# Four banks of depthwise results put into rows by two engines: which engine takes which bank, and in which order

## The chip, the cores and the metric

The kernel runs on one core of one Trainium2 chip. The core has five engines that run side by side and wait for each other through semaphores: TensorE (PE in the profile; its weight loads are PEld), VectorE (DVE), ScalarE (ACT), GpSimd (POOL) and SyncE (SP, which starts transfers). TensorE writes its results into PSUM, 8 banks of 512 float32 values in each of 128 partitions; ScalarE and VectorE read them from there. SBUF is the memory for everything else on the chip. The metric is the device time of the whole program in microseconds, from one launch.

## What is computed

Four layers follow each other, each added to its input: `x = x + layer(group_norm(x))`, with x of shape 2 x 128 x 64 x 64 (two images, 128 channels). Only layer 0 is touched. Its heart, cut from the reference:

```python
xn = biasfree_ln(x, ln1_w)
qkv = conv1x1(xn, w_qkv)                        # 128 -> 640 channels, "pointwise"
qkv = conv_general_dilated(qkv, w_dw, ...,      # 3 x 3, each channel by itself, "depthwise"
                           padding='SAME', feature_group_count=5 * c)
q1, k1, v, q2, k2 = split(qkv, 5, axis=1)       # 128 channels each
q1, q2, k1, k2 = map(l2norm_tokens, (q1, q2, k1, k2))
attn1 = softmax(q1 k1^T * temperature)          # over the 4096 pixels, 4 heads of 32 channels
out1 = attn1 v
...                                             # channel attention with q2, k2
out = conv1x1(out1 + out2, w_po) ; layer norm ; conv1x1 with w_proj
```

The change concerns how the depthwise results of k1 and q1 get from PSUM into their places in SBUF. No number that is computed changes.

## The kernel before

In layer 0 each group of 128 channels is convolved in two halves of 32 image rows. The pointwise product goes through PSUM into a padded frame in SBUF; the depthwise product works on that frame with 32 x 32 pieces of TensorE: channels `32 r .. 32 r + 31` are multiplied by a diagonal matrix for each of 9 taps, and the result for chunk c (8 image rows, 512 pixels) of channel block r lands in partitions `32 c .. 32 c + 31` of bank r. So the results of four chunks lie in the four quarters of the partitions and have to be put back into rows: that is `in_place`.

```python
def sp():                                # 3 buffers of two PSUM banks each
    return spp.tile([128, 2, CH], F32, tag="sp", name="ps_sp")      # CH = 512
...
def pointwise(pad, grp, half):           # a generator: one yield for each block
    ...                                  # memsets of the frame's edges on GpSimd
    for r0 in range(0, H // 2 + 1, 2 * ROWS):          # 16 rows, 16 rows, 1 row
        n = min(2 * ROWS, H // 2 + 1 - r0)
        ps = sp() if n > 1 else acc(0).rearrange("p (o c) -> p o c", o=1)
        for i in range(0, n, ROWS):
            ...
            nc.tensor.matmul(ps[:, i // ROWS, : rows * W], w_qkv[...], xn[...], start=True, stop=True)   # L1524
        nc.scalar.copy(pad[:, to + r0 : to + r0 + n, 1 : W + 1], ...)                                    # L1531
        yield

def depthwise(grp, pad):
    ps = [sp() for _ in range(2)]
    for t in range(9):
        for c in range(4):
            for r in range(4):
                rows, to = slice(32 * r, 32 * r + 32), slice(32 * c, 32 * c + 32)
                y0 = c * ROWS + t // 3
                nc.tensor.matmul(                                                                        # L1546
                    ps[r // 2][to, r % 2, :].rearrange("p (h w) -> p h w", w=W),
                    diag[rows, grp, t, :],
                    pad[rows, y0 : y0 + ROWS, t % 3 : t % 3 + W],
                    start=(t == 0), stop=(t == 8),
                )
    return ps
...
def in_place(ps, half, out, p):
    for c in range(4):
        for r in range(2 * p, 2 * p + 2):
            cols = slice((4 * half + c) * CH, (4 * half + c + 1) * CH)
            (nc.vector.tensor_copy if r % 2 else nc.scalar.copy)(                                        # L1564
                out[32 * r : 32 * r + 32, cols], ps[p][32 * c : 32 * c + 32, r % 2, :]
            )
```

`convolutions` runs eight steps per image, in the order k1, k1, q1, q1, then q2 and k2 by halves. Each step's program order is the order on every engine (`_in_order`):

```python
order = [(1, 0), (1, 1), (0, 0), (0, 1), (3, 0), (4, 0), (3, 1), (4, 1)]
...
for n, (grp, half) in enumerate(order):
    ps = depthwise(grp, frames.pop(0))
    ...
        following = pointwise(frames[-1], *order[n + 2])     # the frame for the step after next
    if grp >= 3:                                             # q2, k2: whole tiles, rows not undone
        for p in range(2):
            copy(qk[:, grp - 3, 2 * p : 2 * p + 2, :], ps[p])                                            # L1557
        run(following)
        ...
    else:                                                    # k1, q1
        in_place(ps, half, out, 0)
        next(following, None)                                # first pointwise block
        in_place(ps, half, out, 1)
        run(following)                                       # second block, and the single row
        for i in range(2):
            squares(...)                                     # ScalarE, sums of squares                    L1571
    if n == 0:
        for half in range(2):
            run(pointwise(pads[half], 2, half))              # the frames of v
        for _ in range(6):
            next(before, None)                               # finish() of the image before
    elif n == 1:
        run(before)
    ...
    if n == 3: ...                                           # norms of q1 and k1
    for _ in range((0, 0, 3, 3, 4, 4, 4, 0)[n]):
        next(taps, None)                                     # VectorE: depthwise taps of v
```

`finish` of the first image (output projections, transposes, layer norm) is woven into the first two steps of the second image.

Of the kernel before, what the change touches and what calls it, by code (L numbers as in the profile page):

```python
# [1406 lines left out]
def _layer0(ctx, tc, X, a, cst, worst, there, dram):  # L1407
    nc = tc.nc
# [149 lines left out]

    def in_place(ps, half, out, p):

        for c in range(4):
            for r in range(2 * p, 2 * p + 2):
                cols = slice((4 * half + c) * CH, (4 * half + c + 1) * CH)
                (nc.vector.tensor_copy if r % 2 else nc.scalar.copy)(  # L1564
                    out[32 * r : 32 * r + 32, cols], ps[p][32 * c : 32 * c + 32, r % 2, :]
                )

    def squares(pool, t, at):
        junk = pool.tile([128, 2 * CH], F32, tag="junk", name="junk", bufs=1)
# [57 lines left out]
    def convolutions(pool, b, before):  # L1627
# [12 lines left out]
        for n, (grp, half) in enumerate(order):  # L1640
# [5 lines left out]
            if grp >= 3:  # L1646
                if grp == 3:
                    qk = pool.tile([128, 2, 4, CH], F32, tag="qk2", name="qk2", bufs=1)
# [4 lines that stand above are left out]
                    squares(pool, qk[:, grp - 3, r, :], ss2[:, grp - 3, r, half : half + 1])  # L1653
            else:
                out = (q1, k1)[grp]
                in_place(ps, half, out, 0)
                next(following, None)
# [3 lines that stand above are left out]
                    at = 2 * half + i  # L1661
                    squares(
                        pool, out[:, at * 2 * CH : (at + 1) * 2 * CH], ss[:, grp, at : at + 1]
                    )
# [677 lines left out]
```

## Time and profile before

| | |
|---|---|
| median of three runs | 4260.06 us (4249.1 to 4260.55) |
| span of the profiled run | 4250.7 us |
| TensorE busy | 4058.6 us, 95% of the span |
| ScalarE busy | 3342.0 us, 79% |
| VectorE busy | 2187.2 us, 51% |
| copies of line 1564 on ScalarE | 64, median 577 ns, 37.0 us in all |
| copies of line 1564 on VectorE | 64, 687 to 688 ns on average, 44.0 us in all |
| mean granted TensorE clock | 0.978 of full speed |

Layer 0's convolutions stand near 40 to 210 us (first image) and 827 to 1045 us (second image); between and after them lies attention, in which TensorE and ScalarE are both nearly always busy. A group of the profile names the line, the engine, the operation, the tile written and the tile read, the shape and how often. "Idle before, releaser" is the time for which an engine stood still just before an instruction, and the instruction that ended that. Idle time matters only on an engine that sets the end.

### The profile page before, as it was taken

The page shows a single profiled execution, that of the slowest core. Times are in us where ns is not written, and L with a number is a line of the kernel's source. Part 1 is how long each engine was busy: PE and PEld are TensorE (multiplying, and loading weights), DVE is VectorE, ACT ScalarE, POOL GpSimd, SP SyncE. Part 2 cuts the span into 40 slices and gives each one's busy share as a digit, 9 for nine tenths or more (in the row PEclk, how much of TensorE's full clock was granted, in tenths as well). Part 3 has the DMA queues.
Part 4 walks back from the last instruction along what each step waited for, and adds up shares of the span by engine and source line. Part 5 has one row for each costly group of instructions (what it writes and reads, how often), then busy time and mean ns, then how long its engine had stood idle before and what let it go on. Part 6 is the DMA issues. An engine that isn't in the chain of part 4 may idle for free. (4 is left out here: it accounts for less than half of the span.)

```text
span 4250.7 us, 82260 instructions
## 1 busy us (share of the span) xinstructions
PE 4058.6 (95%) x35790; PEld 1552.1 (37%) x35790; DVE 2187.2 (51%) x2358; ACT 3342.0 (79%) x4051; POOL 70.4 (2%) x145
## 2 busy tenths in 40 slices
PE   7899999978999998997998999999999999999998
PEld 4523222245222223445665333333333333333332
DVE  3679999746999998986765211321032012211111
ACT  4478888734888884335655999999999999999998
POOL 1001000000000001000000000000000000000000
PEclk9999999999999999998999999999999999999999
DMA  1099970000000000003660000000000000000000
GB/s 48 2 194 191 182 89 1 1 1 2 1 1 1 1 1 12 1 1 128 270 263 4 6 6 4 6 6 4 6 6 6 4 6 6 6 4 6 6 6 4
DMA packets 158822, 158.86 MB, mean 37 GB/s; under 512 B 24809, under 2 KB 148713, under 8 KB 154354
## 3 DMA queue, kind: packets, MB, share of 16 engines
q1 hardware_dynamic: 158450, 153.50, 15.5%
q8 instruction: 282, 4.62, 0.4%
q14 instruction: 90, 0.74, 0.1%
HBM read 145.09 MB, written 73.40 MB: 51 GB/s over the span
## 5 line engine op out<-in xcount | busy, mean ns | idle before, releaser
L2104 ACT ACTIVATE weights<-ps_s 128x1024 f32<-128x1024 f32 x2048 | 1885.2, 1103 | 65.9 <-PE ps_s L2094 65.4
L1350 ACT ACTIVATE weights<-ps_s 128x1024 f32<-128x1024 f32 x1024 | 992.6, 1022 | 175.5 <-PE ps_s L1341 150.6
L2113 PE MATMUL ps_acc<-weights,vt 128*32 128x512 f32 x8192 | 1095.6, 607 | 0.0
L2094 PE MATMUL ps_s<-q,k 32*128 32x512 f32 x8192 | 925.9, 445 | 5.3 <-ACT weights L2104 5.3
L1792 DVE TENSOR_TENSOR sums<-sums,weights 128x2048 f32<-128x2048 f32 x384 | 879.1, 2289 | 42.2 <-ACT weights L1350 6.6
L2094 PEld LDWEIGHTS ps_s<-q,k 32*128 32x128 f32 x8192 | 472.6, 183 | 841.9 <-ACT weights L2104 775.2
L1341 PE MATMUL ps_s<-q,k 32*128 32x512 f32 x4096 | 647.4, 642 | 3.7 <-ACT weights L1350 1.3
L2135 DVE COPY u<-ps_acc 128x512 f32<-128x512 f32 x32 | 22.1, 692 | 1041.5 <-PE ps_acc L2113 1041.5
L1757 PE MATMUL ps_acc<-weights,vt 128*32 128x512 f32 x4096 | 548.8, 605 | 3.4 <-ACT used L1782 3.2
L1341 PEld LDWEIGHTS ps_s<-q,k 32*128 32x128 f32 x4096 | 210.4, 183 | 429.7 <-issue 209.9
L2113 PEld LDWEIGHTS ps_acc<-weights,vt 128*32 128x32 f32 x8192 | 163.2, 108 | 378.8 <-issue 366.8
L1757 PEld LDWEIGHTS ps_acc<-weights,vt 128*32 128x32 f32 x4096 | 81.0, 108 | 395.1 <-issue 377.0
L662 DVE SCALAR_TENSOR_TENSOR X<-g,w,X 128x2048 f32<-128x2048 f32 x84 | 197.4, 2351 | 2.6
L1792 DVE TENSOR_TENSOR sums<-weights 128x2048 f32<-128x2048 f32 x64 | 146.6, 2290 | 63.1 <-ACT weights L1350 63.1
L1546 PE MATMUL ps_sp<-pad,diag 32*32 32x512 f32 x4608 | 165.3, 600 | 4.6 <-DVE q L1564 3.1
L1008 PE MATMUL ps_z<-w_ri,e 128*32 128x128 f32 x2048 | 137.5, 409 | 14.4 <-DVE e L950 12.2
L2055 DVE TENSOR_TENSOR vt<-ps_acc,bv 128x384 f32<-128x384 f32 x32 | 17.8, 557 | 247.1 <-PE ps_acc L2048 247.1
L1524 PE MATMUL ps_sp<-xn,w_qkv 128*128 128x512 f32 x160 | 91.3, 709 | 33.5 <-DVE k L1564 16.0
L1546 PEld LDWEIGHTS ps_sp<-pad,diag 32*32 32x32 f32 x4608 | 95.1, 103 | 62.6 <-issue 15.4
L2025 DVE LOAD_MASK_SELECT qq<-ps_acc x32 | 0.4, 14 | 222.2 <-PE ps_acc L2022 222.2
L2138 DVE RECIPROCAL r<-r 128x512 f32<-128x512 f32 x32 | 107.3, 3353 | 1.1
L950 DVE TENSOR_SCALAR e<-ps_pe 32x136 f32<-32x136 f32 (+1 forms) x352 | 104.4, 297 | 5.0
(288 smaller groups left out, 2602.6 us busy)
## 6 DMA issues: line engine op xcount, KB each, us to landing
w_ri<-w_r SPq DMA_DIRECT2D x16, 2112.0 KB, 8.2
w_ri<-w_i SPq DMA_DIRECT2D x16, 2112.0 KB, 13.5
w_r<-in_L_conv_kr_w SPq DMA_DIRECT2D x15, 528.0 KB, 12.5
w_r<-in_L_conv_kr_x SPq DMA_DIRECT2D x15, 528.0 KB, 12.2
w_r<-in_L_conv_kr_y SPq DMA_DIRECT2D x15, 528.0 KB, 12.1
w_r<-in_L_conv_kr_z SPq DMA_DIRECT2D x15, 528.0 KB, 12.4
w_i<-in_L_conv_ki_w SPq DMA_DIRECT2D x15, 528.0 KB, 12.7
w_i<-in_L_conv_ki_x SPq DMA_DIRECT2D x15, 528.0 KB, 12.2
```

The costliest lines, as they stand in the source:

```text
L662: nc.vector.scalar_tensor_tensor(xi, g[:, i : i + H // 2, j : j + W], w8[:, s : s + 1], xi, ALU.mult, ALU.add)
L950: nc.vector.tensor_scalar_mul(out, got[of, :, s], sign)
L1008: nc.tensor.matmul(out.rearrange("p (n f o) -> p n f o", n=2, f=2), e[:, s, 2 * j : 2 * j + 2, :].rearrange("p f x -> p (f x)"), w.rearran ...
L1341: nc.tensor.matmul(ps[j // 2][:, j % 2, :], k[rows, kt * 128 : (kt + 1) * 128], q[rows, qb * CH : (qb + 1) * CH], start=True, stop=True,)
L1350: nc.scalar.activation(w[:, 2 * p : 2 * p + 2, :], ps[p], AF.Exp)
L1546: nc.tensor.matmul(ps[r // 2][to, r % 2, :].rearrange("p (h w) -> p h w", w=W), diag[rows, grp, t, :], pad[rows, y0 : y0 + ROWS, t % 3 : t ...
L1757: nc.tensor.matmul(ac[n][rows, :], lhs(rows), w[:, j, :], start=first, stop=last)
L1792: nc.vector.tensor_add(parts[0].rearrange("p j c -> p (j c)"), t.rearrange("p j c -> p (j c)"), w.rearrange("p j c -> p (j c)"),)
L2094: nc.tensor.matmul(ps[j // 2][:, j % 2, :], k[rows, kt * 128 : (kt + 1) * 128], q[n][rows, qb * CH : (qb + 1) * CH], start=(n == 0), stop= ...
L2104: nc.scalar.activation(w[p], ps[p], AF.Exp)
L2113: nc.tensor.matmul(ac[0][32 * j : 32 * j + 32, :], vt[:, kt, j // 2, i : i + 2, :].rearrange("p a d -> p (a d)"), w[j // 2][:, i, :], star ...
L2138: nc.vector.reciprocal(r, r)
```

## The change

Before, `in_place(…, p)` handles tile p: its bank 0 goes to ScalarE, its bank 1 to VectorE, chunk by chunk, the same chunk of columns on both. After, ScalarE takes both banks of the first tile and VectorE both banks of the second: call p moves bank p of each tile. VectorE begins two chunks ahead, so the two engines never write the same columns at the same time. The aim is that each engine works through a tile of its own.

```diff
     def in_place(ps, half, out, p):
 
-        for c in range(4):
-            for r in range(2 * p, 2 * p + 2):
+
+        for i in range(4):
+            for n, engine in enumerate((nc.scalar.copy, nc.vector.tensor_copy)):
+                r, c = 2 * n + p, (i + 2 * n) % 4
                 cols = slice((4 * half + c) * CH, (4 * half + c + 1) * CH)
-                (nc.vector.tensor_copy if r % 2 else nc.scalar.copy)(
-                    out[32 * r : 32 * r + 32, cols], ps[p][32 * c : 32 * c + 32, r % 2, :]
-                )
+                engine(out[32 * r : 32 * r + 32, cols], ps[n][32 * c : 32 * c + 32, p, :])
```

The copies are as many as before and of the same shape, eight on each engine in each of the four steps of an image.

## The prediction, made before the changed kernel was run

> **What bounds the kernel now.** I read the page first. TensorE is busy 95% of the span, and in the slices that hold layer 0's convolutions (slice 0 and slices 8 to 9) it is as busy as elsewhere, so any gain has to come out of TensorE's waits there. The group list of line 1564, the line that changes, shows who waits for it:
>
> ```profile
> L1564 ACT COPY k<-ps_sp x32: 573/577/580, 58.1 to 911.1; 32x512 f32<-32x512 f32 x32
> L1564 DVE COPY k<-ps_sp x32: 680/686/698, 58.7 to 911.8; 32x512 f32<-32x512 f32 x32
> ...
> who waited for it (us, times):
>   DVE k L1564: 82.8, 32
>   DVE q L1564: 46.6, 32
>   PE ps_sp L1524: 30.0, 8
> ...
>   PEld ps_sp L1546: 8.8, 5
>   PE ps_sp L1546: 3.9, 5
> ```
>
> Columns of the first lines are shortest/median/longest ns. The two engines wait for each other at every copy, and TensorE's lines 1524 (pointwise) and 1546 (depthwise) wait for the copies. The eight waits of line 1524 are one for each of the eight calls of the depthwise step that end in `in_place`: four per image. The timeline of the second of them, from the end of its depthwise matmuls at 84.53, shows the whole pattern (start us, duration us, engine, line, operation; in brackets idle before it and what ended that idle):
>
> ```profile
> 84.53 1.98 PE L1524 MATMUL ps_sp<-xn,w_qkv 128*128 128x512 f32 x4
> 84.60 0.57 ACT L1564 COPY k<-ps_sp 32x512 f32<-32x512 f32 x1 [8.69 <-PE ps_sp L1546]
> 85.21 0.68 DVE L1564 COPY k<-ps_sp 32x512 f32<-32x512 f32 x1 [16.16 <-ACT k L1564]
> 85.93 0.58 ACT L1564 COPY k<-ps_sp 32x512 f32<-32x512 f32 x1 [0.75 <-DVE k L1564]
> ...
> 89.19 1.01 ACT L1531 COPY pad<-ps_sp 128x1024 f32<-128x1024 f32 x1
> 89.20 0.69 DVE L1564 COPY k<-ps_sp 32x512 f32<-32x512 f32 x1 [0.65 <-ACT k L1564]
> ...
> 90.04 3.13 PE L1524 MATMUL ps_sp<-xn,w_qkv 128*128 128x512 f32 x4 [3.52 <-DVE k L1564]
> ...
> 94.83 0.70 DVE L1564 COPY k<-ps_sp 32x512 f32<-32x512 f32 x1 [0.65 <-ACT k L1564]
> ...
> 95.58 9.72 PE L1546 MATMUL ps_sp<-pad,diag 32*32 32x512 f32 x284 [0.80 <-DVE k L1564]
> ```
>
> ScalarE and VectorE never overlap on these copies: one pair costs 1.33 us (84.60 to 85.93). Four pairs must end before TensorE may start the second pointwise block (90.04), four more before the next depthwise block runs (95.58). Depthwise end to depthwise start is 95.58 - 84.53 = 11.05 us. A step without `in_place` shows what the same TensorE work takes when nothing holds it:
>
> ```profile
> 146.62 3.70 PE L1524 MATMUL ps_sp<-xn,w_qkv 128*128 128x512 f32 x8
> 150.16 0.33 PE L1524 MATMUL ps_acc<-xn,w_qkv 128*128 128x64 f32 x2
> 150.42 1.14 PE L1546 MATMUL ps_sp<-pad,diag 32*32 32x512 f32 x32
> ```
>
> There the gap is 150.42 - 146.62 = 3.80 us. So 7.25 us of such a gap is waiting, or slow matmuls after waiting.
>
> **What the Trainium skill says.** "PSUM — Partial Sum Buffer", section on PSUM bank collisions: ScalarE and VectorE must be kept apart where they touch one bank in the same 32 partitions; different banks are free. The old pair already read two different banks, so the alternation is not needed by the banks; it comes from both engines reading one and the same two-bank tile (at the first copy after the tile changes, ScalarE waits for nobody). The order of instructions with their waits, of both kernels, confirms it: in the changed kernel no copy waits for the other engine any more. Same page, Specifications: both engines read PSUM at full bandwidth together when they don't collide. The trace agrees: whole-tile copies of line 1557 take 1.01 us on ScalarE and 1.22 on VectorE when they run together (186.41 and 186.54), as long as when alone. "TensorE: Matmul & The Clock Gate", What's actually happening: about 3.4 us of idleness drops TensorE to half clock. The trace agrees: after 3.52 us idle the four matmuls at 90.04 took 3.13 us, after 1.16 us (907.19) 1.98 us; after 2.14 us (836.81), partly slow, 2.45.
>
> **The change part by part.** Instruction counts, shapes and TensorE's order stay the same; eight copies per engine and step remain.
>
> Removed: the cross waits. ScalarE's own rate is read from line 691, the same 32x512 copy sixteen times in a row: 9.45 us / 16 = 0.591 each. VectorE's is its 0.687 plus the same 0.014, 0.70.
>
> Moved: the release of buffers. Before, the first tile was free after half the copies; now both are free only at the end. But the order of releases becomes: the buffer of the first pointwise block (free when its copy to the pad is done), then ScalarE's tile, then VectorE's. I take it that buffers are handed out in order of release, as the waits of both kernels fit. So the second pointwise block no longer waits for depthwise copies at all, only for ScalarE's pad copy, which stands after ScalarE's first four copies.
>
> One step, counted from the depthwise end:
> - ScalarE: starts at 0.08, four copies to 0.08 + 4 x 0.591 = 2.45, pad copy 1.02 to 3.47, four more to 5.85.
> - TensorE: first pointwise 0 to 1.98, waits for the pad copy to 3.53 (1.55 idle instead of 3.52, so I expect full speed), second pointwise 1.85, small one 0.26 (both from the free step: 150.16 - 146.62 is 3.54 for two, and 150.42 - 150.16), ends at 5.64.
> - VectorE: starts near 0.2, eight copies of 0.70, ends at 5.8.
> - Next depthwise block: first tile is ScalarE's (5.85), second VectorE's (5.8), with about 0.1 for the handover: 5.95.
>
> So 11.05 becomes 5.95: 5.1 us less. Such gaps are the second, third and fourth step of the first image and the third and fourth of the second: 5 x 5.1 = 25.5 us.
>
> First step of each image (a value pad follows): depthwise ends at 58.06, the next starts at 74.85, 16.79 us. ScalarE is the last there: its squares began at 69.36, after alternating to 68.33, and the value-pad copies follow the squares. ScalarE now finishes copies at 5.85, pad copy 2 at 6.97, squares near 7.1 instead of 11.30. Everything behind them moves by 4.2 us. Twice: 8.4, of which I count 8 since the second image has the latency chain of `finish` behind it, which moves along but may not move whole.
>
> Second step of the second image: a tile of `finish` holds the third buffer, so the first pointwise block waits even now (5.43 us idle, until 902.28). It will then wait for VectorE's eight copies, 5.8: no gain. But the second block need not wait for the pad copy and the transposes that started at 912.51, 15.7 us after the depthwise end, come after 5.8 + 3.75 (slow) + 1.98 + 0.33 = 11.9, or when ScalarE's tile is free: pad copy 9.6 to 10.6, four copies to 13.0. Gain 2.6 to 3.8, I take 3.
>
> Added: in step four the squares end later relative to the next depthwise block, and with them VectorE's norm and its three taps, so the copy of line 1557 (already 1.8 us late at 148.44) comes about 0.9 later; some 0.3 us each, -0.6.
>
> Sum: 25.5 + 8 + 3 - 0.6 = 36 us, out of layer 0 only; attention and the later layers keep their durations and start earlier. Against the median of 4260.06 this gives 4224; against the lowest run, 4249.1, it gives 4213. I say 4221.
>
> **The rivals.** (a) *The later release takes the gain back.* If the second pointwise block gets ScalarE's tile instead of the pad's buffer, it waits until 5.9, longer than the 5.5 of before, TensorE goes slow (3.4 us), and the next depthwise block starts near 9.7. Gain 1.4 x 5 + 8 + 1 = 16 us, 4243. For it: the waits listed name only the engine (ScalarE), which fits both. Against it: in the kernel before, the third step's first tile waits for ScalarE and starts early (93.42), which only a hand-out in order of release explains. (b) *Copies slow each other.* If both engines at once take 20% longer, each step loses about 1.1 us: 5 x 1.1 + 2 x 1 = 8 us of the gain, 4230. Line 1557 speaks against it. (c) *The end is elsewhere.* If the second image's `finish` chain or a weight load set the pace, the gain there vanishes: about 11 us less, 4232. The waits of line 1524 stand on the chain of TensorE, 95% busy, so I give this little. (d) *More gain:* VectorE's successive copies overlap by 0.08 (as line 1833 starts 0.61 after line 1470's 0.69), or `finish` gains more: up to 42 us, 4216.
>
> **Range and chances.** (a) at its worst, with the spread of 11 us of the runs before, gives about 4245; the full gain from the lowest run with some more gives 4205. Low 4204, high 4240. 2% would be 85 us; all waits for line 1564 on TensorE together are 43 us with slow matmuls on top, so 2% can't be reached: faster 0.02, same 0.97, slower 0.01.
>
> **What would show it.** Right: no waits between ScalarE and VectorE on the copies; eight VectorE copies in a row in about 5.6 us; the wait of line 1524 near 1.5 us and its four matmuls 1.98; depthwise gaps of 6 us, 12.5 in the first step. Rival (a): line 1524 idles about 4 us and takes over 3. Rival (b): copies longer than 0.577 and 0.687. Wrong altogether: if depthwise gaps shrink as said but the span does not.

## The result, and the profile after

The changed kernel takes 4225.19 us (median of 4 runs, 4223.08 to 4228.96), the kernel before 4255.27 us (median of 4 runs beside it): a ratio of 0.9928 with a 95% interval of 0.9913 to 0.9943. That is 30 us less, where the prediction said 36 and a time of 4221, range 4204 to 4240. In the profiled runs the span went from 4250.7 to 4221.3 us, at a mean granted TensorE clock of 0.978 and 0.980.

The group list of the line that changed (now line 1566) answers to the one shown of before. Durations are shortest/median/longest ns, then first and last start.

```profile
L1566 ACT COPY k<-ps_sp x32: 575/578/581, 59.2 to 888.4; 32x512 f32<-32x512 f32 x32
L1566 DVE COPY k<-ps_sp x32: 681/688/698, 59.3 to 880.9; 32x512 f32<-32x512 f32 x32
...
its engine sat idle before it (us, times) until:
  PE ps_sp L1546: 156.6, 16
who waited for it (us, times):
  PE ps_sp L1524: 6.3, 3
  PE ps_sp L1546: 1.6, 5
  PEld ps_sp L1524: 0.7, 2
```

The copies last what they lasted before, and no copy waits for the other engine: all 16 waits ahead of copies are for TensorE's depthwise matmuls. TensorE's line 1524 waited for these copies 8 times and 30.0 us; now it is 3 times and 6.3 us, nearly all of it one wait of 5.80 us in the second image. The other seven waits became waits of 1.51 to 1.53 us for the copy to the pad, which this list does not hold.

The timeline of the second depthwise step, from the end of its matmuls at 82.19 (start us, duration us, engine, line, operation; in brackets the idle time before it and what ended it):

```profile
82.19 1.98 PE L1524 MATMUL ps_sp<-xn,w_qkv 128*128 128x512 f32 x4
82.27 2.35 ACT L1566 COPY k<-ps_sp 32x512 f32<-32x512 f32 x4 [8.69 <-PE ps_sp L1546]
82.33 5.61 DVE L1566 COPY k<-ps_sp 32x512 f32<-32x512 f32 x8 [17.43 <-PE ps_sp L1546]
...
84.64 1.01 ACT L1531 COPY pad<-ps_sp 128x1024 f32<-128x1024 f32 x1
85.67 2.36 ACT L1566 COPY k<-ps_sp 32x512 f32<-32x512 f32 x4
...
85.70 1.98 PE L1524 MATMUL ps_sp<-xn,w_qkv 128*128 128x512 f32 x4 [1.52 <-ACT pad L1531]
...
87.52 0.33 PE L1524 MATMUL ps_acc<-xn,w_qkv 128*128 128x64 f32 x2
...
88.18 1.16 PE L1546 MATMUL ps_sp<-pad,diag 32*32 32x512 f32 x32 [0.32 <-ACT k L1566]
```

Both engines start together and each runs through its own tile. The second pointwise block waits 1.52 us for the copy to the pad, not 3.52 us for VectorE, and its four matmuls take 1.98 us, not 3.13. The next depthwise block starts 88.18 - 82.19 = 5.99 us after the last one's end, not 11.05.

The windows over the first image's convolutions tell how much of the gain is waiting and how much is clock (columns: window, its length, busy us of PE, PEld, DVE, ACT and POOL with instruction counts, then TensorE's granted clock, share of the DMA engines, GB/s). First before, then after:

```profile
40.00:211.00 171.00, 148.84 (x2558) 86.09 (x2556) 77.48 (x70) 69.51 (x121) 4.26 (x26) 0.94 0.01 2
```

```profile
40.00:191.00 151.00, 138.01 (x2557) 82.54 (x2556) 77.01 (x70) 70.23 (x121) 4.75 (x26) 1.00 0.01 2
```

TensorE's idle time fell from 22.2 to 13.0 us, 9.2 less. The same matmuls keep it busy for 10.8 us less, and not all of that is clock, though the clock rose from 0.94 to 1.00. Line 1524 is busy for 5.0 us less (46.33 to 41.33) and lines 1608 and 1618 for 1.9 us less (17.63 to 15.76); before, these ran slow after waits. Line 1546 is busy for 3.5 us less (82.54 to 79.09), and most of that is waiting under another name: before, three depthwise blocks began with four matmuls alone, 1.36, 1.15 and 1.05 us long, while the other 284 waited for VectorE. The last 0.5 us is where the windows are cut. So of 20 us gained here about a third is clock. The part of lines 1608 and 1618 need not come from the change: the wait ahead of them is 3.08 us in both kernels, and in the second image they ran slow in both.

### The profile page after: what moved, and what is told of

The parts are those of the page before. It is cut to its first block, busy times and chain, and to the rows that moved or that the text cites. A ratio compares the mean times of both kernels' runs of the same rounds, so it can differ in the third digit from the quotient of the medians.

```text
span 4221.3 us, 82246 instructions
## 1 busy us (share of the span) xinstructions
PE 4050.3 (96%) x35790; PEld 1548.6 (37%) x35790; DVE 2186.7 (52%) x2358; ACT 3342.7 (79%) x4051; POOL 71.6 (2%) x145
## 5 line engine op out<-in xcount | busy, mean ns | idle before, releaser
L948 ACT ACTIVATE e<-ps_pe 32x136 f32<-32x136 f32 (+1 forms) x352 | 99.4, 282 | 4.1
## 6 DMA issues: line engine op xcount, KB each, us to landing
w_r<-in_L_conv_kr_y SPq DMA_DIRECT2D x15, 528.0 KB, 12.3
```

## The experiments

Ten runs, each with the change or the kernel before as its base. "Step" is one depthwise block with what follows it; "gap" is the time from the end of a depthwise block to the start of the next.

**Without the distance of two chunks.** Base: after.

```diff
-                r, c = 2 * n + p, (i + 2 * n) % 4
+                r, c = 2 * n + p, i
```

> The changed kernel without the two chunks' distance: both engines write the same columns (other rows) at the same time. Theory (a tile of its own for each engine ends the waiting; the distance does nothing): no waits between the copies, 0.578 and 0.688 us each, gap from depthwise end to depthwise start 5.97 us as in the changed kernel, ratio to before 0.993. Rival (the distance is needed, because equal columns hold one engine up): copies longer than 0.6 and 0.7 us or waits back, gap above 6.5 us, ratio 0.995 to 1.000.

Measured: 4224.1 us, ratio to before 0.9924 (0.9908 to 0.9941), the same as the change. The second step's gap is 5.99 us (81.15 to 87.14), the copies take 578 and 688 ns. What follows: the distance does nothing that shows, and the gain comes with the tile that each engine has for itself.

**The distance without the own tile.** Base: before. Both engines still read one tile, VectorE two chunks ahead.

```diff
-        for c in range(4):
+        for i in range(4):
             for r in range(2 * p, 2 * p + 2):
+                c = (i + 2 * (r % 2)) % 4
```

> The kernel before with the two chunks' distance alone: VectorE's bank two chunks ahead, both engines still on one tile. Theory (the shared tile makes them alternate): all waits stay, pair 1.33 us, gap 11.05 us, ratio 1.000. Rival (equal columns make them alternate): waits gone, gap near 6 us, ratio 0.993.

Measured: 4257.19 us, ratio 1.0003 (0.9994 to 1.0012). The timeline of its second step shows the wait of before:

```profile
90.19 3.75 PE L1524 MATMUL ps_sp<-xn,w_qkv 128*128 128x512 f32 x4 [3.52 <-DVE k L1565]
```

VectorE's copies into k again wait 82.8 us for ScalarE in 32 waits, to the tenth what they waited before (those into q 48.2 us, where it was 46.6). Together the two runs settle what made the engines alternate: they read one tile. The columns they write play no part.

**All copies before the first pointwise block.** Base: after. Here ScalarE's tile and VectorE's are both ahead of the pad copy in the order of release, which makes a case like the one that rival (a) described.

```diff
                 in_place(ps, half, out, 0)
-                next(following, None)
                 in_place(ps, half, out, 1)
+                next(following, None)
                 run(following)
```

> The changed kernel with all copies ahead of the first pointwise block in program order, so that ScalarE's tile is released before the pad's buffer and its pad copy comes last. Theory (the order in which buffers come free is a part of the gain): the second pointwise block waits for ScalarE's eighth copy, starts at 4.9 us instead of 3.5 after the depthwise end, idle 2.9 us before it, gap 7.0 us at full TensorE clock and up to 8.5 when the clock drops; 6 to 12 us of the 30 are lost, 4231 to 4237 us. Rival (only the parallel copies count): gap 6.0 us, as the changed kernel.

Measured: 4233.65 us, ratio 0.9945 (0.9928 to 0.9961): some 9 us slower than the changed kernel (4225.19, and 4224.1 without the distance). TensorE's timeline of the second and the fourth step:

```profile
83.88 1.98 PE L1524 MATMUL ps_sp<-xn,w_qkv 128*128 128x512 f32 x4
88.70 1.98 PE L1524 MATMUL ps_sp<-xn,w_qkv 128*128 128x512 f32 x4 [2.84 <-ACT k L1566]
90.53 0.33 PE L1524 MATMUL ps_acc<-xn,w_qkv 128*128 128x64 f32 x2
90.78 9.77 PE L1546 MATMUL ps_sp<-pad,diag 32*32 32x512 f32 x288
...
117.09 1.98 PE L1524 MATMUL ps_sp<-xn,w_qkv 128*128 128x512 f32 x4
121.93 3.47 PE L1524 MATMUL ps_sp<-xn,w_qkv 128*128 128x512 f32 x4 [2.86 <-ACT q L1566]
...
125.50 9.76 PE L1546 MATMUL ps_sp<-pad,diag 32*32 32x512 f32 x288
```

Now the second pointwise block waits for a tile of depthwise results, 2.84 to 2.86 us, and in these two steps its matmuls once stayed fast and once ran slow: gaps of 6.90 and 8.41 us. So the second block takes the buffer that was released first, as the prediction supposed; in the change that is the pad's, and this order is worth some 9 of the 30 us. The traces agree: from the end of the first depthwise block to the start of the attention, the two images take 7.0 and 3.1 us more than in the change.

**The squares later.** Base: after. In the first step ScalarE's sums of squares stand behind the pointwise blocks of the value pads, not ahead of them.

```diff
                 in_place(ps, half, out, 1)
                 run(following)
+            if n == 0:
+                for h in range(2):
+                    run(pointwise(pads[h], 2, h))
+            if grp < 3:
                 for i in range(2):
                     squares(...)
             if n == 0:
-                for half in range(2):
-                    run(pointwise(pads[half], 2, half))
                 for _ in range(6):
```

> The changed kernel with ScalarE's sums of squares behind the value-pad copies in the first step of each image. Theory after the trace (TensorE's own pointwise matmuls set that step, 7.46 us without a wait after the copies): first gap 13.35 us as before this edit. Theory of the prediction (ScalarE sets it): squares moved out of the way, gap 11 us.

Measured in a single run: 4207.31 us. But the first gap, which this edit is about, is the same as in the change to the hundredth: 13.35 us.

```profile
57.64 1.99 PE L1524 MATMUL ps_sp<-xn,w_qkv 128*128 128x512 f32 x4
...
70.99 1.47 PE L1546 MATMUL ps_sp<-pad,diag 32*32 32x512 f32 x33
```

So ScalarE does not set the end of the first step after the change, and the 18 us of the whole must come from elsewhere. In the trace, 8.4 us of them lie behind the second image's convolutions (3200.2 us to the end of the span, in the change 3208.6) and 3.6 us in the first image's attention (617.2 against 620.8), which the edit does not touch. The kernel was run again; the 14 us that the expectation names fit this run's time set against the changed kernel's span of 4221.3 us:

> The same edit as in the one look before, timed, because that look ended 14 us below the changed kernel although the gap that the edit aims at was the same 13.35 us. Theory (the 14 us came from stretches in which TensorE happened to be granted a higher clock, 0.984 against 0.980 over the whole run, and are no effect of the edit on layer 0): layer 0's gaps as in the changed kernel; the time between 4215 and 4228, ratio 0.991 to 0.993. Rival (the edit itself brings it): 4205 to 4210, ratio 0.989.

Measured: 4216.93 us, with runs from 4208.07 to 4221.98, ratio 0.9908 (0.9886 to 0.993), whose interval overlaps the change's. Its profiled run has the same gap, 13.34, and a span of 4220.2 us at a clock of 0.979, where the single run had 4205.5 at 0.984. One kernel, 15 us apart: a single whole time says nothing about an edit of a few microseconds here. If a small gain hides in the 4217, this doesn't tell.

**Finish runs nine steps in the first, not six.** Base: after. `finish` of the first image then holds no two-bank buffer while it pauses for the second step's depthwise block; with six steps it holds one of the three.

```diff
-                for _ in range(6):
+                for _ in range(9):
                     next(before, None)
```

> The changed kernel with nine instead of six steps of finish in the first step of the second image, so that no tile of finish holds the third buffer in the second step. Theory (that buffer costs the second step 5.8 us of waiting and slow matmuls after it): from the first depthwise end to the third depthwise start of the second image 73.65 us become 66 to 68, the first pointwise block of the second step starts at once, the time falls to 4217 to 4220, ratio 0.991 to 0.992. Rival (finish's own chain of latencies sets that stretch, and the moved steps cost the same elsewhere): 73 us stay, ratio 0.993.

Measured: 4212.16 us (4212.03 to 4214.46), ratio 0.9897 (0.988 to 0.9913), 13 us faster than the change: this version beats both kernels. From the end of the first depthwise block of the second image to the start of the third it takes 896.61 - 832.18 = 64.43 us; in the change it is 906.26 - 832.61 = 73.65. First the change, then this kernel, both from TensorE's timeline:

```profile
865.44 10.48 PE L1546 MATMUL ps_sp<-pad,diag 32*32 32x512 f32 x288
881.72 6.46 PE L1524 MATMUL ps_sp<-xn,w_qkv 128*128 128x512 f32 x8 [5.80 <-DVE k L1566]
...
888.18 0.60 PE L1816 MATMUL ps_sp<-consts,y 128*128 128x128 f32 x4
890.17 1.12 PE L1821 MATMUL ps_acc<-yn,w_pr 128*128 128x512 f32 x2 [1.38 <-ACT pad L1531]
...
904.29 2.04 PE L1821 MATMUL ps_acc<-yn,w_pr 128*128 128x512 f32 x2 [0.94 <-DVE X L1833]
906.26 10.51 PE L1546 MATMUL ps_sp<-pad,diag 32*32 32x512 f32 x288
```

```profile
876.00 9.77 PE L1546 MATMUL ps_sp<-pad,diag 32*32 32x512 f32 x288
885.70 1.98 PE L1524 MATMUL ps_sp<-xn,w_qkv 128*128 128x512 f32 x4
889.21 1.98 PE L1524 MATMUL ps_sp<-xn,w_qkv 128*128 128x512 f32 x4 [1.53 <-ACT pad L1531]
...
895.55 1.13 PE L1821 MATMUL ps_acc<-yn,w_pr 128*128 128x512 f32 x2 [1.68 <-ACT yn L1818]
896.61 9.76 PE L1546 MATMUL ps_sp<-pad,diag 32*32 32x512 f32 x288
```

In the change the held buffer costs an idle of 5.80 us and then eight matmuls at 6.46 us; without it both blocks run at full speed and the tail of `finish` as well. The first step grows by 11 us for it, the second shrinks by 20. That is 9.2 of the 13 us; about 4 lie outside this stretch and are not explained.

**The same nine steps with the old copies.** Base: before.

> The kernel before with nine instead of six steps of finish in the first step of the second image. Theory (the held buffer is a cost of its own, and part of it hides behind alternating copies): from the first depthwise end to the third depthwise start of the second image 78.63 us become about 73, the gaps stay 11.05, the time falls by 5 to 6 us, ratio 0.9987. Rival (the whole 9.2 us that the nine steps brought on the changed kernel come back): 69.4 us, ratio 0.9978. Rival (the nine steps help only the changed kernel): 78.6 us, ratio 1.000.

Measured: 4254.03 us against 4250.65 of before, ratio 1.0009 (1.0 to 1.0018). In the profile the stretch shrinks from 78.63 to 73.19 us, as expected, and the next attention starts at 1039.34, not 1043.36; but the time doesn't show it. Right behind the stretch 1.7 us are given back, since the third depthwise block takes 11.46 us, not 9.76. The runs spread over 17 us (4242.31 to 4259.39), and where the rest of the 5 us went stays open.

**Eleven steps.** Base: after, `range(11)`: all of `finish` in the first step.

> The changed kernel with all eleven steps of finish in the first step of the second image. Theory (with nine, the last two steps cost 5 us in the second step, with waits for ScalarE's squares; in the first step they cost their own latencies of some 4 us): the second step's gap becomes 6 us, the stretch of 64.43 us becomes 63 to 64.5, the time equals that of nine steps, 4211 to 4213, ratio 0.989 to 0.990. Rival (latencies of the last steps are fully exposed in the first step): 68 us, 4216.

Measured: 4220.64 us, ratio 0.993 (0.9913 to 0.9947), above both expectations; the stretch is 66.78 us, between the two. So the stretch explains 2.4 of the 8.5 us by which this kernel is slower than the one with nine steps; in the two profiles 6.3 us lie behind the second image's convolutions, which the edit does not touch. The last steps of `finish` are a chain from engine to engine with no second chunk beside it, as the idle before its last transposes shows:

```profile
875.93 1.11 PE L1816 MATMUL ps_sp<-consts,y 128*128 128x128 f32 x4 [2.47 <-DVE y L1470]
880.72 9.76 PE L1546 MATMUL ps_sp<-pad,diag 32*32 32x512 f32 x288
```

With nine steps this tail lies beside the second step's copies. So more is not always better: of the three counts run, nine is the one where the buffer is free and the tail still has company.

**Nine steps and the squares later.** Base: after, both edits.

> Both edits, nine steps of finish and late squares, on the changed kernel. Theory (squares off TensorE's path bring nothing, nine steps bring 9 us in their stretch): as nine steps alone, 4208 to 4216, ratio 0.989 to 0.991. Rival (both edits bring their own share): 4195 to 4200, ratio 0.986.

Measured: 4213.19 us (4210.8 to 4213.79), ratio 0.9904 (0.9886 to 0.9923), as with nine steps alone. The squares bring nothing that can be seen.

**One VectorE copy more.** Base: after. VectorE does its last copy of each step twice (the second time writes the same values).

```diff
-                engine(out[...], ps[n][...])
+                for _ in range(2 if n == 1 and p == 1 and i == 3 else 1):
+                    engine(out[...], ps[n][...])
```

> The changed kernel with VectorE's last copy of each step done twice (nine copies on VectorE instead of eight; the result is the same). Theory (VectorE's and ScalarE's copies both end within 0.1 us of the next depthwise start and set it): gap 5.97 becomes 6.5 to 6.65 us. Rival (TensorE's own pointwise work sets it, done at 5.65): gap 6.0 us.

Measured in a single run: 4230.12 us. The timeline of the second step:

```profile
81.46 1.98 PE L1524 MATMUL ps_sp<-xn,w_qkv 128*128 128x512 f32 x4
...
81.58 6.33 DVE L1567 COPY k<-ps_sp 32x512 f32<-32x512 f32 x9 [16.74 <-PE ps_sp L1546]
...
87.43 10.68 PE L1546 MATMUL ps_sp<-pad,diag 32*32 32x512 f32 x288 [0.32 <-ACT k L1567]
...
88.37 0.25 PEld L1546 LDWEIGHTS ps_sp<-pad,diag 32*32 32x32 f32 x32 [0.81 <-ACT pad L1531]
```

The depthwise block starts after 5.97 us, as in the change and not after 6.5 as expected, and then stalls: its weight loads wait 0.81 us until 88.37 for ScalarE's second pad copy, though VectorE's ninth copy is done at 87.91. The block takes 10.68 us instead of 9.76. From block end to block end that is 0.9 us more for 0.7 us of copy, so VectorE has no slack here, as the theory said, though the time is lost inside the block. Why ScalarE ends the stall is an argument and not shown: VectorE's tile now comes free after the pad's, and the hand-out order turns, so that the block's second tile is the pad's buffer.

## Why the prediction was right, and which terms were not

*Five gaps of 11.05 us become 5.95: 25.5 us.* Right. Measured are 5.97 to 5.99 us, in all 5.06 + 5.08 + 5.07 + 5.06 + 5.06 = 25.3 us. Each link stands in the second step's timeline: ScalarE's four copies in 2.35 us, VectorE's eight in 5.61 (predicted 5.6), the wait 1.52 (1.55), the matmuls at full speed.

*Rival (a), a later release.* Out: the wait is for the pad copy, and the run that made the depthwise tiles the ones waited for was 9 us slower. *Rival (b), copies that slow each other.* Out: 578 and 688 ns, where 577 and 686 to 687 stood before. *Rival (c), the end elsewhere.* Out for the five gaps, partly right for the second image, as its second step shows below. *Rival (d)* asked for 42 us; none of it came, and VectorE's eight copies did not overlap (5.61 us).

*The first step of each image: 4.2 us each, "ScalarE is the last there".* Mis-sized, and for a wrong reason. Measured are 16.79 to 13.35 us in the first image and 36.23 to 32.83 in the second: 3.44 + 3.40 = 6.8 us of the 8. In the first image the end of this step is TensorE's, and was so before the change. There it ran the value pads' pointwise blocks from 67.12 to 74.85 without idle time (its weight loads waited once, 0.88 us), and ScalarE's last copy waited for TensorE:

```profile
67.12 3.97 PE L1524 MATMUL ps_sp<-xn,w_qkv 128*128 128x512 f32 x8
...
71.10 3.65 PE L1524 MATMUL ps_sp<-xn,w_qkv 128*128 128x512 f32 x8
...
74.79 1.01 ACT L1531 COPY vpad<-ps_sp 128x1024 f32<-128x1024 f32 x1 [0.24 <-PE ps_sp L1524]
...
74.85 9.75 PE L1546 MATMUL ps_sp<-pad,diag 32*32 32x512 f32 x288
```

After the change:

```profile
59.16 1.98 PE L1524 MATMUL ps_sp<-xn,w_qkv 128*128 128x512 f32 x4
62.67 1.98 PE L1524 MATMUL ps_sp<-xn,w_qkv 128*128 128x512 f32 x4 [1.53 <-ACT pad L1531]
...
65.05 3.70 PE L1524 MATMUL ps_sp<-xn,w_qkv 128*128 128x512 f32 x8 [0.23 <-ACT k L1566]
...
68.76 3.65 PE L1524 MATMUL ps_sp<-xn,w_qkv 128*128 128x512 f32 x8
...
72.51 9.76 PE L1546 MATMUL ps_sp<-pad,diag 32*32 32x512 f32 x288
```

The same blocks run from 65.05 to 72.51, 7.46 us where it was 7.73. So the step gained what the start of these blocks gained, from 9.06 us after the depthwise end (58.06 to 67.12) to 5.89 (59.16 to 65.05), and 0.27 us less in the blocks themselves. The prediction moved ScalarE's end and did not lay TensorE's own matmuls of the step end to end; had it done so, its 5.85 us for ScalarE's tile and the 7.73 us of before would have given a gap of 13.6 us. Moving the squares, which left the gap as it was, shows that ScalarE is not the bound in the changed kernel.

*The second step of the second image: 3 us.* The mechanism was right, the size wasn't. The transposes of line 1816 came 12.3 us after the depthwise end (875.92 to 888.18) instead of 15.7, so 3.5 us were gained there, but the gap fell only from 32.00 (896.77 to 928.77) to 30.34 (875.92 to 906.26): 1.7 us. The rest was given back behind the transposes. Line 1821 then waits 1.38 us for the pad copy, and its last two calls run slow, 2.04 us instead of 1.10.

*Steps four and five: -0.6 us.* Did not show. The gap behind the fifth depthwise block of an image is 3.80 us (129.20 to 133.00), as before. VectorE's copy did come 0.6 us later (2.41 us after the depthwise end, before 1.82), but TensorE did not wait for it.

The terms measured in place make 25.3 + 6.8 + 1.7 = 33.8 us. The mechanism carries the number: three quarters of it come from the term that was right to 0.2 us, and the two mis-sized ones were 2.5 us too high together. The two profiled spans differ by only 29.4, and the missing 4.4 us, which no term foresaw, are spread over stretches that the change does not touch: the start is 1.1 us later (first depthwise end 58.06 and 59.16), layer 0's attention of the first image takes 620.8 us instead of 617.7, all the rest after the second image's convolutions 1.25 us more; within the convolutions some small pieces went about 1 us the other way. That in the attention is mostly TensorE's clock. The windows around the place where it slows, before and then after:

```profile
291.00:312.00 21.00, 19.24 (x118) 5.92 (x114) 12.66 (x21) 14.07 (x17) 1.56 (x2) 0.92 1.11 192
```

```profile
272.00:296.00 24.00, 22.24 (x117) 6.09 (x114) 12.77 (x21) 13.96 (x17) 1.56 (x2) 0.79 1.18 197
```

The same 117 or 118 matmuls take 3.0 us more at a clock of 0.79 than at 0.92. Whether these 4 us of attention and rest are chance or go with the change stays open: the same attention took 617.2 to 620.7 us in the other runs, without a rule that I could see. So the prediction's step "attention and the later layers keep their durations" holds only to a few microseconds.

Two readings were off without harm. TensorE is not as busy in the slices of layer 0's convolutions as elsewhere: the page has 7, 7 and 8 tenths for slices 0, 8 and 9, where most others have 9. And the 43 us behind the remark on 2% add weight loads that wait beside the matmuls; TensorE's matmuls alone waited 30.0 + 3.9 + 3.2 = 37.1 us for line 1564.

## What to carry to other kernels

In this program two engines that read different banks of one tile were kept apart; where each has its own tile they run side by side, and that nearly halved a gap that recurs five times. Before saying which engine ends a stage, lay the work of *every* engine in it end to end, for the one with the last visible wait need not be the one that sets the end. After taking a wait away, ask in which order the buffers come free. When buffers pass between interleaved pieces of work, a piece that holds one while it pauses can cost more than the copies; and edits worth a few microseconds are judged by the stretch they touch, not by a whole time that wanders by 15.

## What the runs showed of the hardware

I had expected a clear length of idle time above which TensorE slows down. None shows in these runs. In the gaps behind depthwise blocks, four pointwise matmuls took 1.98 or 1.99 us after waits of 1.5 us and over 3 us after 3.52 us, but in between both occur. With all copies ahead of the first pointwise block, seven waits of 2.84 to 2.86 us were followed by 1.98 us twice and by 3.20 to 3.56 us five times. The wait of 2.14 us that the prediction calls partly slow (2.45 us) recurs as 2.13 us in the changed kernel, and there the four matmuls took 1.98. The changed kernel has that wait, and the wait of 3.08 us once in each image with both outcomes:

```profile
151.38 1.16 PE L1618 MATMUL ps_acc<-tok 128*128 128x128 f32 x8 [3.08 <-ACT tok L1557]
...
820.83 1.98 PE L1524 MATMUL ps_sp<-xn,w_qkv 128*128 128x512 f32 x4 [2.13 <-ACT pad L1531]
...
970.22 2.08 PE L1618 MATMUL ps_acc<-tok 128*128 128x128 f32 x8 [3.08 <-ACT tok L1557]
```

The Trainium skill, "TensorE: Matmul & The Clock Gate", section What's actually happening, states that activity is judged over a window of 3413 ns that runs freely, and that the point at which the clock comes up depends on where in the window the first matmul lands. Read so, the moment of the idle time counts beside its length. The lines above agree with that, but no run here moved the moment alone. It could also be why one kernel ran in 4208 and in 4222 us, which is not shown.
